# A selective scan with attention and experts behind it: the last direction of three batches is scanned in two halves of the positions, six sums change engine, and ties are drawn from another seed

## The chip, the cores and the metric

One Trainium2 chip, one core. The time is device microseconds (us) of one execution. An execution under the profiler has a time of its own, given below beside the runs without it.

## The reference, cut to what matters

The input is a 4 x 384 x 32 x 32 image; all arithmetic is float32. Layer 0 normalises it in groups and runs a state-space scan over the 1024 positions in four directions (rows forward, columns forward, and both reversed); layer 1 is windowed causal attention and a top-2-of-4 mixture of experts over the 1024 tokens of each batch:

```python
x_dbl = einsum('bkdl,kcd->bkcl', xs, x_proj_weight)      # k: 4 directions
dt = softplus(einsum(..., dts, dt_projs_weight) + bias)
h = h * exp(dt * A) + (dt * u) * B                       # 384 channels x 16 states
y = (h * C).sum(states)                                  # over 1024 positions
x = x + gelu(layernorm(merge of the 4 directions + D * u))
t = t + attention(layernorm(t))                          # 6 heads, window 64, causal
t = t + sum over 2 of 4 experts of gate * (gelu(t @ w1 + b1) @ w2 + b2)
```

The layer norm, and so attention, needs the sum of all four directions at a position. Attention is causal, so the first 512 tokens of a batch don't need the last 512.

## The kernel before, in words

**The scan.** There are 16 turns: four batches of four directions each, in `ORDER` (columns forward, columns reversed, rows forward, rows reversed). A turn has 48 slots. A slot is one tile of 128 partitions (32 channels x 4 states) by 1024 positions; 12 blocks `n` of channels by 4 groups `g` of states make a turn, and `place_of` takes two blocks at a time. For each slot, in the order of `s`:

- `spread` (twice, for the decay and for the input) brings a block's rows of `dtr` from DRAM to 128 partitions, each row copied to four partitions (tiles `dts` and `dtu`; the profile calls both dts);
- `times_b` on GpSimd makes z = dt * u times B;
- `decay` on ScalarE makes dA = exp(scale * dt) into PSUM, of which there are two buffers of this shape;
- `scan` on VectorE runs the recurrence over the 1024 positions, into dA or into z;
- `times_c` multiplies by C, on VectorE or, where the recorder's clocks say that GpSimd is less far along, on GpSimd;
- `fold_y` adds up the 16 states on TensorE with a 128 x 32 matrix of ones, four matmuls for each pair of slots, and adds the result to the rows of `ydr`.

`time_steps` and `half_step` make `dtr` ahead of that: a small matmul, five ScalarE passes and some VectorE passes over 128 x 512 pieces. In the turns of batch 0 (`by_pe`) the three parts of dt are summed by TensorE with an identity matrix; in the others by two VectorE operations.

**Attention.** `layer1` waits until all four directions of a batch have been added (`("scan", b) in have`) and then runs `tokens(b)`: eight tiles of 128 tokens, three at a time, with transposes, norms, projections, scores and outputs on TensorE and copies and norms on ScalarE and VectorE.

**Experts.** `route` orders the tokens of half a batch (four tiles) by expert. The experts' work is 73 blocks of 128 tokens for one expert each, in `hidden` (36 matmuls of 128 x 128 a block, tile ps_hid) and `output` (12 matmuls of 128 x 384 a block, tile y_ff); the profile shows each fp32 matmul as two records. In order of half batches the blocks are 5 and 14 (batch 0), 5 and 8 (batch 1), 8 and 14 (batch 2), 5 and 14 (batch 3). A block can run when its half batch has been routed. `combine` gathers the two experts' rows, weights and adds them and writes the output.

**The order of the work.** The program is straight-line. A recorder (`Machine`) runs these generators against a model of the engines and writes each engine's instructions in the order that it finds; on the chip each engine goes through its list in that order. A request with the bias `EARLY` (the scan's supply, folds, attention, routes) goes ahead of one with `LATER` (experts, combine). Requests that are equal are ordered by a small random amount, from the fixed `SEED`. Nothing is decided at run time but the experts' numbers and the tokens' addresses.

Of the kernel before, what the change touches and what calls it, by code (L numbers as in the profile page):

```python
# [11 lines left out]
F32 = mybir.dt.float32  # L12
AF = mybir.ActivationFunctionType
# [4 lines left out]
P = 128  # L18
# [371 lines left out]


PATIENCE = 3.0
TIE, SEED = 0.1, 53
SOON = 0.5
WINDOW, COLD = 3.413, 1.9
MARGIN, QUEUES = 1.0, ("sp",)
# [4 lines left out]
def conv_attn_hybrid(  # L401
# [88 lines left out]
    count_p = const.tile([P, SEG], F32, name="count_p")  # L490
    base_of = [const.tile([P, NE], F32, name=f"base{n}") for n in range(min(2, len(PACKS)))]
    a4 = const.tile([P, KG, T, JB, NG], F32, name="a4")

    m = Machine(nc)
    ps_a = ctx.enter_context(tc.tile_pool(name="ps_a", bufs=1, space=PSUM))
# [64 lines left out]
    zs, das, ready = {}, {}, set()  # L560
# [4 lines left out]
    def place_of(s):  # L565

        return s // SP * 2 + s % 2, s % SP // 2

    def scans(n):
        return lambda: count_of["scan"] >= n  # L570
# [272 lines left out]
    def time_steps():  # L843

        for i, (b, k) in enumerate(turns):
            for t in range(T):
                yield lambda: i in xds and i in dtws and (i == 0 or ("u", b) in have) and count_of["scan"] >= (i * T + t) * TS - 40
                if i:
                    u = yield from us_all.take("ub")
                    yield from sp.dma_start(u, udr[b][t])  # L850
                else:
                    u = first_u[t][:, :L]
                dtr = dram.tile([2, P, L], F32, tag="dtr", name="dtr", bufs=4)
                halves_ = [half_step(i, t, h, u, dtr) for h in range(NH)]
                yield from m.together(halves_, 1 if b else NH, EARLY)
                if i:
                    us_all.give(u)
                dtrs[i, t] = dtr
            if i == KG - 1:
                own_ = lambda: [f for f in eds.free if f[1].startswith("pt")]  # L860
                yield lambda: len(own_()) == 3
                pts_.free += own_()
                eds.free = [f for f in eds.free if f not in pts_.free]

    def half_step(i, t, h, u, dtr):
        b, k = turns[i]
        bias, c = dtb_sb[:, k, t : t + 1], ts(h, HB)
        by_pe = b == 0
        e, dt, *more = yield from eds.take("ed", n=3 if by_pe else 2)
        w = yield from banks.take("ps_dt", 0)  # L870
        yield from pe.matmul(w, dtws[i][h][:, ts(t, P)], xds[i][h], start=True, stop=True)
        yield from act.activation(e, w, AF.Abs, bias=bias)
        yield from act.activation(dt, w, AF.Relu, bias=bias)
        yield from act.activation(e, e, AF.Exp, scale=-1.0)
        if by_pe:
            yield from act.activation(w, e, AF.Identity, bias=minus, scale=-1.0)
            yield from dve.scalar_tensor_tensor(e, w, 1.0, e, ALU.add, ALU.add)
            yield from act.activation(more[0], w, AF.Ln, scale=-1.0)
            mm = Calls()
            for n, part in enumerate((dt, e, more[0])):  # L880
                mm.matmul(w, ident, part, start=n == 0, stop=n == 2)
            yield from pe.all(mm)
        else:
            yield from act.activation(w, e, AF.Identity, bias=1.0)
            yield from dve.scalar_tensor_tensor(e, w, -1.0, e, ALU.add, ALU.subtract)
            yield from act.activation(w, w, AF.Ln)
            yield from dve.tensor_tensor(w, w, e, ALU.subtract)
            yield from dve.tensor_tensor(w, w, dt, ALU.add)
        if k % 2:
            v = slice(h * (WW // NH), (h + 1) * (WW // NH))  # L890
            yield from dve.tensor_tensor(
                e.rearrange("p (w h) -> p w h", h=HH),
                w.rearrange("p (w h) -> p w h", h=HH), colmajor(u)[:, v, :], ALU.mult,
            )
        else:
            yield from dve.tensor_tensor(e, w, u[:, c], ALU.mult)
        yield from act.copy(dt, w)
        banks.give(w)
        yield from sp.dma_start(dtr[1][:, c], e)
        yield from sp.dma_start(dtr[0][:, c], dt)  # L900
        eds.give(e, dt, *more)

    def spread(c):

        for n, (i, t, j) in enumerate(blocks):
            yield lambda: (i, t) in dtrs
            dst = yield from (dtus if c else dts).take("dts")
            yield from sp.dma_start(
                dst, dtrs[i, t][c, 32 * j : 32 * j + 32, :].unsqueeze(1).to_broadcast([32, SG, L])
            )  # L910
            spreads[n, c] = dst

    def times_b():
        for s in range(NSLOT):
            n, g = place_of(s)
            i = blocks[n][0]
# [4 lines left out]
            yield from pool.tensor_tensor(z, spreads[n, 1], bcs[i, g, 0], ALU.mult)  # L921
            zs[s] = z
            count_of["times"] += 1
            if g == NG - 1:
                dtus.give(spreads.pop((n, 1)))
            if n % NB == NB - 1:
                bs_.give(bcs.pop((i, g, 0)))

    def decay():
        for s in range(NSLOT):  # L930
            n, g = place_of(s)
            i, t, j = blocks[n]
            yield lambda: (n, 0) in spreads and "a4" in have
            da = yield from das_.take("dA")
            yield from act.activation(
                da, spreads[n, 0], AF.Exp, scale=a4[:, turns[i][1], t, j, g : g + 1]
            )
            das[s] = da
            if g == NG - 1:
                dts.give(spreads.pop((n, 0)))  # L940

    def times_c(s, h, on_pool):
        n, g = place_of(s)
        i = blocks[n][0]
        yield lambda: (i, g, 1) in bcs
        if on_pool:
            yield from pool.tensor_tensor(zs[s], zs[s], bcs[i, g, 1], ALU.mult)
        else:
            yield from dve.tensor_tensor(zs[s], h, bcs[i, g, 1], ALU.mult)
            das_.give(h)  # L950
        if n % NB == NB - 1:
            cs_.give(bcs.pop((i, g, 1)))
        ready.add(s)

    def scan():

        for s in range(NSLOT):
            n, g = place_of(s)
            i = blocks[n][0]
# [4 lines left out]
            if turns[i][1] >= 2:  # L964
                yield from dve.tensor_tensor_scan(
                    h[:, ::-1], da[:, ::-1], z[:, ::-1], 0.0, ALU.mult, ALU.add
                )
            else:
                yield from dve.tensor_tensor_scan(h, da, z, 0.0, ALU.mult, ALU.add)
            count_of["scan"] = s + 1  # L970
            if s % SP == 0:
                m.spawn(fold_y(n), EARLY)
            if on_pool:
                das_.give(da)
                m.spawn(times_c(s, h, True))
            else:
                yield from times_c(s, h, False)
# [11 lines left out]
    def fold_y(n):  # L989


        i, t, j = blocks[n]
        b, k = turns[i]
        rows_y = ydr[b][t, j : j + 2].rearrange("j r l -> (j r) l")
# [77 lines left out]
    def tokens(b):  # L1072
# [241 lines left out]
    def route(at_part):  # L1314
# [67 lines left out]
        nb = rp.tile([P, NE], F32, tag="nb", name="nb")  # L1382
        slot = rp.tile([P, PT, NE], F32, tag="slot", name="slot", bufs=1)
        if opens:
            total = rp.tile([P, NE], F32, tag="total", name="total")
            done = rp.tile([P, NE], F32, tag="done", name="done")
            start = rp.tile([P, NE], F32, tag="start", name="start")
# [325 lines left out]
```

## Time and profile before

| | |
|---|---|
| three runs | 3725.29, 3725.83 and 3727.22 us; median 3725.83 us |
| profiled execution | 3715.52 us; span of the core 3713.8 us; mean granted TensorE clock 0.852 |
| busy in the span | TensorE 2999.4 us (81%), VectorE 2858.1 (77%), GpSimd 2802.2 (75%), ScalarE 2217.3 (60%) |
| DMA | 944.51 MB, mean 254 GB/s |

The span has three stages. Up to about 740 us only the scan of batch 0 and its preparation run. From there to the last scan's end, at 3030 us, the scans of batches 1 to 3 run beside the attention and the experts of the batches before. After that only attention of batch 3, the experts that are left and the output remain; VectorE and GpSimd are nearly idle there.

In the pages and answers, a group's line gives engine, operation, tile written and tiles read, and count, then busy us and mean ns of one; a window's line gives each engine's busy us and instructions in that stretch, the granted TensorE clock as a share of full speed, the share of the DMA engines that was busy and their GB/s. L155 and L166 are the recorder's own lines, through which nearly all instructions go, so instructions are told apart by their tiles.

### The profile page before, as it was taken

To read this page: it belongs to the slowest core of one execution; us is meant where nothing else is said; L and a number is where in the kernel's file an instruction comes from. 1 tells how busy PE (TensorE), PEld (TensorE's weight loads), DVE (VectorE), ACT (ScalarE), POOL (GpSimd) and SP (SyncE) were. 2 spreads that over 40 slices of the span, in tenths; PEclk is the share of its full clock that TensorE was granted. 3 is DMA by queue.
4 is the path that set the end of the run, shared out by engine and by line. 5 is a ranking of instruction groups with operands and counts; after the bars stand their busy time and mean duration, and the time that the engine had idled before them with its cause. 6 is when DMAs were issued, how large, how long until landed. Compare 5 with 4: busy or idle time off the path is not lost.

```text
span 3713.8 us, 49879 instructions
## 1 busy us (share of the span) xinstructions
PE 2999.4 (81%) x15793; PEld 1820.8 (49%) x15793; DVE 2858.1 (77%) x3282; ACT 2217.3 (60%) x3984; POOL 2802.2 (75%) x1466
## 2 busy tenths in 40 slices
PE   5566565578788888896778898988888889999997
PEld 2111110045455545463445555655555558877886
DVE  4999999989888999999888999898898963331001
ACT  4454455477676777775667577876667644542221
POOL 3999988989899988999888799998899950112001
PEclk8766776688799989896778899987999999999997
DMA  5876887635489988864369999553899874469995
GB/s 201 288 279 238 276 301 251 207 124 165 150 298 347 368 323 329 304 211 151 124 218 311 328 338 347 194 178 133 291 320 328 321 262 156 153 222 321 321 322 174
DMA packets 396472, 944.51 MB, mean 254 GB/s; under 512 B 50064, under 2 KB 181256, under 8 KB 396208
## 3 DMA queue, kind: packets, MB, share of 16 engines
q1 hardware_dynamic: 384600, 915.73, 70.7%
q0 software_dynamic: 8192, 25.17, 2.0%
q8 instruction: 126, 2.06, 0.2%
q14 instruction: 138, 1.13, 0.1%
q10 hardware_dynamic: 3416, 0.41, 0.1%
HBM read 765.26 MB, written 194.77 MB: 259 GB/s over the span
## 4 chain that ended last, share of the span: by engine, by line
PE 34%; DVE 14%; ACT 10%; POOL 8%; DMA 7%; issue 6%; SPq 1%; another core or an unknown queue 1%; DVEq 0%; POOLq 0%; ACTq 0%
PE y_ff L166 9%; PE ps_hid L166 9%; POOL z L155 6%; DVE dA L155 5%; DVE z L155 4%; PE ps_y L166 3%; PE ps_qk L166 3%; ACT dA L155 2%; PE ps_pr L166 2%; DMA dtr<-ed 2%; PE ps_o L166 2%; ACT ed L155 1%; DVE ps_r L166 1%; PE ps_c L166 1%; ACT L166 1%
## 5 line engine op out<-in xcount | busy, mean ns | idle before, releaser
L155 POOL TENSOR_TENSOR z<-dts,bc 128x1024 f32<-128x1024 f32 x768 | 1792.9, 2363 | 112.5 <-PE ps_y L166 55.7
L155 ACT ACTIVATE dA<-dts,a 128x1024 f32<-128x1024 f32 x768 | 855.3, 1118 | 500.5 <-DVE z L155 486.0
L155 DVE TENSOR_TENSOR_SCAN dA<-dA,z 128x1024 f32<-128x1024 f32 x418 | 955.9, 2287 | 88.9 <-ACT dA L155 75.1
L166 PE MATMUL ps_y<-z,fold 128*32 128x512 f32 x3072 | 665.9, 732 | 321.4 <-POOL z L155 177.1
L155 POOL TENSOR_TENSOR z<-z,bc 128x1024 f32<-128x1024 f32 x350 | 821.3, 2360 | 106.7 <-DVE z L155 105.3
L155 DVE TENSOR_TENSOR_SCAN z<-dA,z 128x1024 f32<-128x1024 f32 x350 | 786.3, 2275 | 38.3 <-ACT dA L155 36.2
L166 PE MATMUL y_ff<-w_sb,hs 128*128 128x384 f32 x1752 | 671.1, 524 | 49.7 <-ACT hs L166 48.6
L166 PEld LDWEIGHTS ps_hid<-xbt,w_sb 128*128 128x128 f32 x5256 | 634.5, 196 | 131.0 <-issue 47.5
L166 PE MATMUL ps_hid<-xbt,w_sb 128*128 128x128 f32 x5256 | 658.8, 282 | 23.1 <-DMA w_sb<-wl 6.7
L155 DVE TENSOR_TENSOR z<-dA,bc 128x1024 f32<-128x1024 f32 x418 | 510.3, 1221 | 19.1
L166 PEld LDWEIGHTS y_ff<-w_sb,hs 128*128 128x128 f32 x1752 | 333.9, 204 | 297.9 <-ACT hs L166 72.9
L155 ACT ACTIVATE hs<-ps_hid,bb 128x128 f32<-128x128 f32 x876 | 262.0, 365 | 337.8 <-PE ps_hid L166 249.6
L166 PEld LDWEIGHTS ps_y<-z,fold 128*32 128x32 f32 x3072 | 91.6, 118 | 694.6 <-POOL z L155 322.9
L155 POOL DMA_INDIRECT cb<-ysdr,idx x64 | 61.9, 967 | 311.8 <-DMA ysdr<-yb 277.1
L166 POOL TENSOR_TENSOR rn<-rn,half 128x1 f32<-128x1 f32 x96 | 53.1, 553 | 229.6 <-DVE rn L166 188.3
L155 DVE COPY yb<-y_ff 128x384 f32<-128x384 f32 x23 | 12.8, 557 | 243.6 <-PE y_ff L166 242.0
L155 POOL DMA_INDIRECT xsdr<-tks,idx x64 | 65.4, 1022 | 110.0 <-DVE idx L166 48.2
L155 ACT ACTIVATE ed<-ps_dt,dtb_sb 128x512 f32<-128x512 f32 x192 | 123.5, 681 | 38.0 <-PE ps_dt L155 24.1
L155 ACT COPY ed<-ps_dt 128x512 f32<-128x512 f32 x96 | 56.2, 585 | 116.0 <-DVE ed L155 115.8
L166 PE MATMUL ps_dt<-ed,ident 128*128 128x512 f32 x144 | 82.7, 729 | 45.0 <-ACT ed L155 45.0
L155 PE MATMUL ps_dt<-xd,dtw_sb 12*128 12x512 f32 x180 | 108.7, 780 | 9.3 <-DVE gate L166 3.0
L311 ACT ACT_TABLE_LOAD x79 | 101.4, 1283 | 13.0 <-DMA gb_sb<-in_gb_dram 11.6
(220 smaller groups left out, 3509.8 us busy)
## 6 DMA issues: line engine op xcount, KB each, us to landing
w_sb<-wl SPq DMA_DIRECT2D x584, 576.0 KB
dts<-dtr SPq DMA_DIRECT2D x384, 512.0 KB
bc<-xdr SPq DMA_DIRECT2D x128, 512.0 KB
dtr<-ed SPq DMA_DIRECT2D x192, 256.0 KB
yp<-ydr SPq DMA_DIRECT2D x96, 256.0 KB
ydr<-yp SPq DMA_DIRECT2D x96, 256.0 KB
ub<-udr SPq DMA_DIRECT2D x45, 512.0 KB
xsdr<-zero SPq DMA_DIRECT2D x12, 1536.0 KB
```

Of the source, the lines that this page charges most:

```text
L155: return getattr(self.real, op)(*a, **k)
L166: getattr(self.real, op)(*a, **k)
L311: self.nc.scalar.add_instruction(mybir.InstLoadActFuncSet(name=self.nc.get_next_instruction_name(), act_func_set_id=EXP_LN_SET,))
```

## The change

Turns 7, 11 and 15, the last of batches 1, 2 and 3, are scanned in two parts (`halved`): all 384 channels over positions 0 to 511, then all of them over 512 to 1023. A slot still covers 128 partitions and 1024 columns, but these are two blocks of channels by 512 positions. Such a slot has two scans of 512, two exponentials of 512, and spreads of two half-rows each; the state at position 511 is kept in `carry` (a copy of two columns) and is the second part's start. The last direction must then run forward, so `ORDER` ends with rows forward. `layer1` starts a batch when its first 512 positions are complete, and each tile waits for its own half. The six sums of the first piece of the first turn (`by_pe`, i + t = 0) are made by VectorE. The seed for ties is 46, and three small routing tiles have one buffer.

```diff
-TIE, SEED = 0.1, 53
+TIE, SEED = 0.1, 46
...
+    carry = [const.tile([P, 2 * NG], F32, name=f"carry{n}") for n in range(NB // NH)]
...
-    ORDER = (1, 3, 0, 2)
+    ORDER = (1, 3, 2, 0)
...
+    halves = [(c, t, j) for c in range(NH) for t in range(T) for j in range(0, JB, 2)]
+    halved = (7,11,15)
...
+    def what(n):
+        i, t, j = blocks[n]
+        if i not in halved:
+            return i, None, t, j
+        return i, *halves[n - i * NB]
...
+    def rows_of(i, g, c, hf):
+        bc = bcs[i, g, c]
+        return bc if hf is None else bcast(bc[:, ts(hf, HB)], 2)
+    def kept(n, g):
+        return carry[n % NB % (NB // NH)][:, 2 * g : 2 * g + 2].unsqueeze(2)
...
-        by_pe = b == 0
+        by_pe = b == 0 and i + t > 0
...
+            else:
+                for o in range(2):
+                    r = slice(32 * (j + o), 32 * (j + o) + 32)
+                    yield from sp.dma_start(
+                        dst[:, ts(o, HB)],
+                        dtrs[i, t][c, r, ts(hf, HB)].unsqueeze(1).to_broadcast([32, SG, HB]),
+                    )
...
+            for o in range(1 if hf is None else 2):
+                c = slice(0, L) if hf is None else ts(o, HB)
+                yield from act.activation(
+                    da[:, c], spreads[n, 0][:, c], AF.Exp,
+                    scale=a4[:, turns[i][1], t, j + o, g : g + 1],
+                )
...
+        eng = pool if on_pool else dve
+        if hf == 0:
+            yield from eng.tensor_copy(kept(n, g), pairs(h)[:, :, HB - 1 : HB])
+        yield from eng.tensor_tensor(view(zs[s], hf), view(h, hf), rows_of(i, g, 1, hf), ALU.mult)
...
+            if hf is not None:
+                for o in range(2):
+                    c = ts(o, HB)
+                    initial = kept(n, g)[:, o, :] if hf else 0.0
+                    yield from dve.tensor_tensor_scan(h[:, c], da[:, c], z[:, c], initial, ALU.mult, ALU.add)
...
-        folded[b] = folded.get(b, 0) + 2
-        if folded[b] == KG * NB:
-            have.add(("scan", b))
+        key = b, hf
+        folded[key] = folded.get(key, 0) + 1
+        whole = (KG - (i // KG * KG + KG - 1 in halved)) * NB // 2
+        for c in range(NH):
+            if folded[b, None] == whole and (whole == KG * NB // 2 or folded.get((b, c), 0) == NB // 4):
+                have.add(("scan", b, c))
...
         def tile(a):
+            yield lambda: ("scan", b, a // PT) in have
...
-            yield lambda: ("scan", b) in have
+            yield lambda: ("scan", b, 0) in have
             yield from tokens(b)
```

More of the change, by code (lines that the diff above doesn't have):

```diff
@@ L567, in place_of, with pairs, view @@
         return s // SP * 2 + s % 2, s % SP // 2
+    def what(n):
[3 more added lines that the diff above has]
+        return i, *halves[n - i * NB]
+    def pairs(ap):
+        return ap.rearrange("p (o l) -> p o l", o=2)
+    def rows_of(i, g, c, hf):
+        bc = bcs[i, g, c]
+        return bc if hf is None else bcast(bc[:, ts(hf, HB)], 2)
+    def view(ap, hf):
+        return ap if hf is None else pairs(ap)
+    def kept(n, g):
+        return carry[n % NB % (NB // NH)][:, 2 * g : 2 * g + 2].unsqueeze(2)
     def scans(n):
@@ L846, in time_steps @@
             for t in range(T):
-                yield lambda: i in xds and i in dtws and (i == 0 or ("u", b) in have) and count_of["scan"] >= (i * T + t) * TS - 40
+                first = i * IS + t * TS // (2 if i in halved else 1)
+                yield lambda: i in xds and i in dtws and (i == 0 or ("u", b) in have) and count_of["scan"] >= first - 40
                 if i:
@@ L903, in spread @@
     def spread(c):
-        for n, (i, t, j) in enumerate(blocks):
+        for n in range(len(blocks)):
+            i, hf, t, j = what(n)
             yield lambda: (i, t) in dtrs
             dst = yield from (dtus if c else dts).take("dts")
-            yield from sp.dma_start(
-                dst, dtrs[i, t][c, 32 * j : 32 * j + 32, :].unsqueeze(1).to_broadcast([32, SG, L])
-            )
+            if hf is None:
+                yield from sp.dma_start(
+                    dst, dtrs[i, t][c, 32 * j : 32 * j + 32, :].unsqueeze(1).to_broadcast([32, SG, L])
+                )
+            else:
+                for o in range(2):
+                    r = slice(32 * (j + o), 32 * (j + o) + 32)
+                    yield from sp.dma_start(
+                        dst[:, ts(o, HB)],
+                        dtrs[i, t][c, r, ts(hf, HB)].unsqueeze(1).to_broadcast([32, SG, HB]),
+                    )
             spreads[n, c] = dst
@@ L915, in times_b @@
             n, g = place_of(s)
-            i = blocks[n][0]
+            i, hf, *_ = what(n)
             yield lambda: (
@@ L920, in times_b @@
             z = yield from zs_.take("z", 0)
-            yield from pool.tensor_tensor(z, spreads[n, 1], bcs[i, g, 0], ALU.mult)
+            yield from pool.tensor_tensor(
+                view(z, hf), view(spreads[n, 1], hf), rows_of(i, g, 0, hf), ALU.mult
+            )
             zs[s] = z
@@ L931, in decay @@
             n, g = place_of(s)
-            i, t, j = blocks[n]
+            i, hf, t, j = what(n)
             yield lambda: (n, 0) in spreads and "a4" in have
             da = yield from das_.take("dA")
-            yield from act.activation(
-                da, spreads[n, 0], AF.Exp, scale=a4[:, turns[i][1], t, j, g : g + 1]
-            )
+            for o in range(1 if hf is None else 2):
[3 more added lines that the diff above has]
+                    scale=a4[:, turns[i][1], t, j + o, g : g + 1],
+                )
             das[s] = da
@@ L943, in times_c @@
         n, g = place_of(s)
-        i = blocks[n][0]
+        i, hf, *_ = what(n)
         yield lambda: (i, g, 1) in bcs
[L946 to L949, printed above, removed]
+        eng = pool if on_pool else dve
+        if hf == 0:
+            yield from eng.tensor_copy(kept(n, g), pairs(h)[:, :, HB - 1 : HB])
+        yield from eng.tensor_tensor(view(zs[s], hf), view(h, hf), rows_of(i, g, 1, hf), ALU.mult)
+        if not on_pool:
             das_.give(h)
@@ L958, in scan @@
             n, g = place_of(s)
-            i = blocks[n][0]
+            i, hf, *_ = what(n)
             yield lambda: s in zs and s in das
@@ L963, in scan @@
             h = z if on_pool else da
-            if turns[i][1] >= 2:
+            if hf is not None:
[3 more added lines that the diff above has]
+                    yield from dve.tensor_tensor_scan(h[:, c], da[:, c], z[:, c], initial, ALU.mult, ALU.add)
+            elif turns[i][1] >= 2:
                 yield from dve.tensor_tensor_scan(
@@ L989, in fold_y @@
     def fold_y(n):
-        i, t, j = blocks[n]
+        i, hf, t, j = what(n)
         b, k = turns[i]
-        rows_y = ydr[b][t, j : j + 2].rearrange("j r l -> (j r) l")
+        if hf is None:
+            rows_y = ydr[b][t, j : j + 2].rearrange("j r l -> (j r) l")
+        else:
+            rows_y = ydr[b][t, :, 32 * hf : 32 * hf + 32, :]
         yield lambda: ("yd", b, t) in have and "fold" in have
@@ L1384, in route @@
         if opens:
-            total = rp.tile([P, NE], F32, tag="total", name="total")
-            done = rp.tile([P, NE], F32, tag="done", name="done")
-            start = rp.tile([P, NE], F32, tag="start", name="start")
+            total = rp.tile([P, NE], F32, tag="total", name="total", bufs=1)
+            done = rp.tile([P, NE], F32, tag="done", name="done", bufs=1)
+            start = rp.tile([P, NE], F32, tag="start", name="start", bufs=1)
             counts[PACK[b]] = total, done, start
```

## The prediction

> **What bounds the kernel now.** I read the busy times in windows of 50 us first: stages have different limits.
>
> ```profile
> core 0: us, PE busy (x) PEld busy (x) DVE busy (x) ACT busy (x) POOL busy (x), PEclk, DMA share, GB/s
> 1200.00:1250.00 50.00, 46.86 (x274) 29.80 (x274) 45.94 (x46) 36.22 (x59) 49.37 (x23) 0.99 0.93 344
> ...
> 1700.00:1750.00 50.00, 30.76 (x98) 13.47 (x98) 46.37 (x40) 30.73 (x40) 49.39 (x28) 0.50 0.45 147
> ...
> 3500.00:3550.00 50.00, 50.00 (x308) 40.07 (x307) 1.67 (x3) 11.91 (x40) 0.00 (x0) 1.00 0.93 316
> ```
>
> Until 3030 us VectorE (DVE) and GpSimd (POOL) are both over 90% busy in most windows: they set the scan's pace. After it TensorE (PE) alone is full. So the end is the last scan's end, 3030 us, plus the TensorE work still left then, 684 us. The same windows for y_ff show which expert work fills TensorE:
>
> ```profile
> 1500.00:1550.00 50.00, 17.32 (x48) 8.47 (x48) 0.00 (x0) 0.95 (x2) 0.96 0.94 337
> ...
> 1700.00:1750.00 50.00, 0.00 (x0) 0.00 (x0) 0.00 (x0) 0.00 (x0) 0.50 0.45 147
> ...
> 3500.00:3550.00 50.00, 26.32 (x76) 13.12 (x74) 1.67 (x3) 0.00 (x0) 1.00 0.93 316
> ```
>
> Experts run at 1050 to 1650, 1950 to 2400 and from 2600 on. Between, all blocks that have been routed are used up and the next batch's attention is still under way: TensorE is 61% busy at half clock at 1700. Expert work missing from these two holes is done after 3030. That is what the change can move.
>
> Then the groups, for the scan's prices, and the waits:
>
> ```profile
> L155 ACT ACTIVATE dA<-dts,a 128x1024 f32<-128x1024 f32 x768 | 855.3, 1118 | 500.5 <-DVE z L155 486.0
> L155 DVE TENSOR_TENSOR_SCAN dA<-dA,z 128x1024 f32<-128x1024 f32 x418 | 955.9, 2287 | 88.9 <-ACT dA L155 75.1
> ...
> L155 DVE TENSOR_TENSOR_SCAN z<-dA,z 128x1024 f32<-128x1024 f32 x350 | 786.3, 2275 | 38.3 <-ACT dA L155 36.2
> ```
>
> ```profile
> PE ps_y L166 <- POOL z L155: 177.1, 92, 7.1
> PE ps_y L166 <- DVE z L155: 131.3, 76, 4.4
> ```
>
> The scan waits 111 us in all for ScalarE (ACT), that is 0.15 us a slot; folds on TensorE wait 308 us for products.
>
> **1. What moves, by the built order.** The instruction order of both programs can be counted without running them. Ahead of the last fold on TensorE stand 46.25 blocks of y_ff and 47.25 of ps_hid before, 50.0 and 51.0 after: 3.75 more. Attention matmuls of all kinds amount to 24.0 tiles there before, 25.2 after. By half-turns: the first three tiles of batch 1 move from turn 8 into turn 7, no experts stand in turns 9.0 and 9.5 before, 4 blocks after, and batch 1's eight tiles end a full turn earlier. The hole of batch 2 stays two half-turns long but lies one half-turn earlier (12.0 and 12.5 instead of 12.5 and 13.0).
>
> Price of a block after 3030 us: from 3450 to 3650 TensorE does nothing else; the y_ff windows there hold 76 + 76 + 74 + 78 = 304 records, at 24 a block 12.7 blocks in 200 us: 15.8 us. Price of a tile: 684 us less 26.3 blocks x 15.8 = 415, the last 46 us (output after the last block) and 16 combined tiles x 2.45 (the two ps_c rows, 78.5 us for 32) = 39 leaves 184 us for 8 tiles, 23 us each. So the work left falls by 3.75 x 15.8 + 1.2 x 23 = 59 + 28 = **87 us**.
>
> **2. What the moved work costs the scan.** I took the start of every 24th of the 768 scans in the timeline. With nothing beside (turns 0.5 to 3.5) a half-turn takes 81.4 us in the mean; with three blocks beside (6.0 to 7.5, 11.0, 11.5, 14.0, 14.5) 88.9, so 2.5 us a block; with attention of batch 0 (4.0 to 5.0; 7.8 tiles) 315.6, so (315.6 - 244.2 - 2)/7.8 = 8.9 us a tile, of batch 2 (12.0 to 13.5) about 10. The moved work costs 3.75 x 2.5 + 1.2 x 9.5 = **21 us** of later scan end.
>
> **3. What the two parts cost.** 144 slots (3 turns) get a second scan. No scan of 512 is in the trace. Additions of 1024 (1221 ns) against 512 (685, rows of yp and ps_dt) give 2 x 685 - 1221 = 149 ns for one more instruction; scans back to back start every 2.21 us where one alone takes 2.29, which puts the lower end at 80 ns. At 149: 21 us of VectorE. Copies of the state: 46 on VectorE (0.16 us, the row of 128x3 from PSUM: 7 us) and 26 on GpSimd (between 0.19 and 0.55 us, rows of rn; 5 to 14 us). Three products move to GpSimd: +7 us there, -4 on VectorE. An initial value read from a tile instead of a constant is in no row: 0 to 149 ns for each of 144 scans, 0 to 21 us; I take 0, since the VectorE rows whose scalar is a tile (tensor_scalar on rn, 153 ns) are no dearer than others. Together 24 us on VectorE and 17 on GpSimd; these two share the products by their loads, so half the sum, 21 us, if the sharing holds, and 13 to 45 at the ends.
>
> ScalarE: 288 exponentials of 512 for 144 of 1024. Rows of 512 take 0.60 to 0.63, so 2 x 0.61 - 1.12 = 0.10 us a slot, 14 us, nearly all beside the scan (ScalarE is 70 to 75% busy, and idles 486 us waiting for buffers that VectorE frees). But VectorE is queued behind this, so 3 us of it counts. Together **24 us**.
>
> The 72 spreads become 144 with half the bytes each: 72 more issues at 0.52 us on SP's queue, 37 us over 530 us of halved turns; weights and folds' rows are queued behind them. SP's waits are for producers, and spreads run ahead by four buffers, so I take 0. If that cover is gone, a late weight stops ps_hid, which waited 6.7 us for weights in all: up to 10 us. In the trace's packet records, packets of 2048 bytes take 84 ns (median) and of 4096 bytes 159: the same per byte, so nothing is added. *The Trainium skill, "Perfetto Trace Analysis", section "DMA Optimizations", speaks against the change here: it says that batching from 2 KB to 4 KB "can dramatically improve throughput", and the change goes the other way. The packet rows don't bear that out; by the rule the sum would rise, as the third rival works out.*
>
> **4. First sums by VectorE.**
>
> ```profile
> 36.11 7.37 PE L166 MATMUL ps_dt<-ed,ident 128*128 128x512 f32 x12 [2.94 <-ACT ed L155]
> ...
> 40.95 1.03 DVE L155 TENSOR_TENSOR ed<-ps_dt,xn 128x512 f32<-128x512 f32 x1 [2.79 <-PE ps_dt L166]
> ```
>
> The first product waits until 40.95 for TensorE. Two VectorE additions (0.69 each) after the logarithm's end at 36.1 give 37.5. VectorE's other small work of this moment (a, count, base) costs half a us. All of the first spread, which GpSimd waits 35 us for, follows: **-3 us**.
>
> **5. The seed.** It reorders near-equal requests all over the program; its large effects are in the counts of part 1. What is left is put in the range, +-10 us.
>
> **Sum.** Scan's end 3030 - 3 + 21 + 24 = 3072; work behind it 684 - 87 = 597; span 3669, which is 45 less. The profiled execution (3715.5) was 10 us under the median of the other runs; the same difference taken from 3725.8 gives about **3681 us**.
>
> **Rivals.**
> - *Slower: the halved turns starve for dA.* A half-slot needs two exponentials, then two scans, with only two buffers between ScalarE and VectorE, and time steps for all three channel tiles of such a turn fall into its first half. If VectorE stands for six tenths of 1.22 us in each of 144 slots, 105 us stand in place of the 24: 3681 + 81 = 3762. It decides from (45 + 24)/144 = 0.48 us a slot. For it: the 111 us of waits for dA. Against: they are 0.15 us a slot.
> - *Nothing gained: TensorE no longer full behind the scan.* Before the last route of batch 3, 8.25 blocks of y_ff fill gaps between 8 tiles behind the last scan; after, 5 between 6.8 tiles. If a chain of tiles (three at a time, about 75 us from rows to token) sets the pace, half of the 87 is lost: 3725. Against: 5 x 15.8 + 6.8 x 23 = 235 us of work is more than 2.3 rounds x 75 = 170.
> - *Slower: packets.* Spreads of halved turns are 72 x 128 packets of 4 KB, at 187 ns (mean) and over 16 DMA engines 108 us. If halves cost as much as wholes, 108 us are added where the DMA share is 0.85 to 1.0: 3681 + about 70 = 3751. Against: the packet rows.
> - *Faster: the second scans hide.* If the pair overlaps (80 ns), VectorE's added work goes where it stood waiting, and experts in former gaps cost the scan nothing: 10 in place of 45 us: 3646.
>
> **Chances.** Forecast 0.59, faster rival 0.17, nothing gained 0.09, starved 0.12, packets 0.03. About 7.5 us (0.2%) is what a measurement tells from no change. Faster by more than that: 0.59 + 0.17 and a little of "nothing gained", 0.78; within 0.07; slower 0.15. The range runs from the faster rival to just beyond no change, 3645 to 3735; the likeliest case's own is 3663 to 3712, from the unknown costs (-8; +21 and a late weight's 10) and the seed's 10.
>
> **What would show it.** Right: the last scan ends at 3060 to 3085; y_ff windows fill around turn 9 (1700 to 1800 before) and the clock there rises from 0.50; about 23 blocks behind the last scan and some 600 us; 512 scans at 1.2 us; half-turns in turns 7, 11, 15 at 3 to 7 us over their like before. Wrong: scans waiting for dA by well over 111 us; TensorE below 90% between the last scan and the last route; a scan's end after 3110.

## The result and the profile after

The changed kernel takes 3712.1 us (median of 16 runs, 3703.3 to 3721.9), the kernel before 3726.2 us (16 runs, 3710.3 to 3740.3): a ratio of 0.9963, 95% interval 0.9951 to 0.9974. That is 14 us faster, where 45 were forecast. The profiled executions can't show these 14: that of before was 10.6 us under its median, that of after, 3717.15 us (span 3715.4), 5.0 us above its own. Executions of the kernel after lie up to 10 us from their median, of the one before up to 16; a scan's end read from one profile is meant with that error throughout. The chips of e9 to e18 were 0.4% faster for the kernel before too (3711 against 3727 us), so kernels are compared by their ratios. Scan's end and the us behind it from e7 are multiplied by 0.9956 where they stand beside those chips'. That is an assumption: a scan of 1024 takes 2.28 us in the mean on every one of them, so the scan's stage need not shrink by the same share.

In the spans, the last scan ends at 3110.9 us (before: 3029.6; forecast: 3072), and 604.5 us of work follow it (before: 684.2; forecast: 597). The gain behind the scan came as forecast; the scan lost twice what was forecast.

The windows of after that answer to those of before:

```profile
core 0: us, PE busy (x) PEld busy (x) DVE busy (x) ACT busy (x) POOL busy (x), PEclk, DMA share, GB/s
1200.00:1250.00 50.00, 46.89 (x258) 28.62 (x258) 42.63 (x40) 40.85 (x67) 46.58 (x22) 0.93 0.94 334
1700.00:1750.00 50.00, 41.41 (x198) 28.79 (x197) 42.65 (x111) 31.05 (x63) 34.29 (x22) 0.69 0.61 196
3500.00:3550.00 50.00, 50.00 (x305) 39.80 (x304) 1.68 (x3) 12.45 (x42) 0.00 (x0) 1.00 0.93 319
```

and for y_ff alone:

```profile
core 0: us, PE busy (x) PEld busy (x) DVE busy (x) ACT busy (x), PEclk, DMA share, GB/s
1500.00:1550.00 50.00, 6.51 (x18) 3.18 (x18) 0.00 (x0) 0.00 (x0) 1.00 0.78 260
1700.00:1750.00 50.00, 6.20 (x12) 3.16 (x12) 0.00 (x0) 0.00 (x0) 0.69 0.61 196
1800.00:1850.00 50.00, 10.11 (x24) 4.90 (x24) 0.00 (x0) 0.47 (x1) 0.93 0.71 233
3500.00:3550.00 50.00, 26.89 (x78) 13.42 (x76) 1.68 (x3) 0.00 (x0) 1.00 0.93 319
```

At 1700 us TensorE is now 41 of 50 us busy (31 before), at a granted clock of 0.69 instead of 0.50; half a block of y_ff stands in a window that had none, a whole one at 1800. At 1500, where 48 records of y_ff stood, there are now 18. From 3500 on the stage behind the scan is as full as it was. VectorE, 92% busy at 1200 us before, is 85% busy there now; but that window lies in turn 6, which isn't halved, and turns 4 to 6 take 594.4 us from scan start to scan start (before: 598.3). The loss is not there.

What the two parts are made of, in the groups by form (count, then busy us and mean ns of one):

```profile
L155 ACT ACTIVATE dA<-dts,a 128x512 f32<-128x512 f32 x288 | 197.2, 691 | 75.4 <-DVE z L155 70.8
...
L155 DVE TENSOR_TENSOR_SCAN dA<-dA,z 128x512 f32<-128x512 f32 x92 | 112.8, 1226 | 26.9 <-issue 9.3 <-ACT dA L155 8.1 <-POOL z L155 4.4
...
L155 DVE TENSOR_TENSOR_SCAN z<-dA,carry,z 128x512 f32<-128x512 f32 x82 | 100.2, 1265 | 1.5 <-ACT dA L155 1.5
...
L155 DVE TENSOR_TENSOR_SCAN dA<-dA,carry,z 128x512 f32<-128x512 f32 x62 | 79.6, 1285 | 14.8 <-ACT dA L155 5.7 <-POOL z L155 5.2 <-issue 3.0
...
L155 DVE TENSOR_TENSOR_SCAN z<-dA,z 128x512 f32<-128x512 f32 x52 | 59.7, 1202 | 1.4 <-ACT dA L155 0.9 <-DMA w_sb<-wl 0.5
...
L155 DVE COPY carry<-dA 128x2 f32<-128x2 f32 x46 | 7.3, 158 | 1.4
...
L155 POOL COPY carry<-z 128x2 f32<-128x2 f32 x26 | 5.0, 193 | 24.8 <-DVE z L155 24.8
```

The 288 scans of 512 take 352.3 us; 144 of 1024 at 2.28 us would take 329. So VectorE has 23.5 us more of scans and 7.3 of copies (forecast: 21 and 7), GpSimd 5.0 of copies (5 to 14). The exponentials of 512 are dearer than forecast: 691 ns instead of 0.61 us, 197.2 us in place of 144 x 1.118 = 161, so 36 us and not 14 on ScalarE.

The waits (total us, times, longest us):

```profile
PE ps_y L166 <- POOL z L155: 168.0, 72, 7.4
...
PE ps_y L166 <- DVE z L155: 116.6, 66, 5.1
...
DVE dA L155 <- ACT dA L155: 70.8, 49, 4.5
...
DVE z L155 <- ACT dA L155: 32.6, 25, 5.2
```

The scan's waits for dA come to 103 us, against 111 before, and to 16 us in the three halved turns alone, against 15: the halved turns don't starve for it, as the first rival had it. Nor did the folds wait longer (285 us, before 308).

Where, then, does the scan lose? In the halved turns. Half-turns (24 slots) in us, from the starts of the scans; "whole slots" is e6 and "not halved" e5, both below:

| half-turn | before | after | whole slots | not halved |
|---|---|---|---|---|
| 7, first | 87.1 | 102.8 | 85.9 | 86.8 |
| 7, second | 88.6 | 106.6 | 103.9 | 87.9 |
| 11, first | 89.1 | 99.1 | 89.2 | 91.5 |
| 11, second | 85.8 | 108.9 | 102.0 | 88.5 |
| 15, first | 74.8 | 88.4 | 79.9 | 76.2 |
| 15, second | 75.6 | 99.5 | 90.4 | 75.6 |
| sum | 501.1 | 605.3 | 551.2 | 506.5 |

No attention of the batch can stand in the first halves, and yet they are 15.7, 10.0 and 13.6 us longer than before; 3 to 7 were forecast. Turn 7's first half in the windows, before and then after:

```profile
core 0: us, PE busy (x) PEld busy (x) DVE busy (x) ACT busy (x) POOL busy (x), PEclk, DMA share, GB/s
1317.30:1404.40 87.10, 77.99 (x398) 43.41 (x397) 82.49 (x56) 59.91 (x97) 72.33 (x31) 0.91 0.86 306
```

```profile
core 0: us, PE busy (x) PEld busy (x) DVE busy (x) ACT busy (x) POOL busy (x), PEclk, DMA share, GB/s
1316.40:1419.10 102.70, 87.78 (x447) 50.79 (x445) 85.55 (x94) 74.96 (x139) 78.68 (x42) 0.93 0.92 320
```

15.6 us more time, but only 3.1 more of work on VectorE and 6.4 on GpSimd. VectorE's idle time rises from 4.6 to 17.2 us, GpSimd's from 14.8 to 24.0. This half-turn is long because both engines that carry the scan wait more, not because they do more. That doesn't hold for all six: a table below has VectorE's busy and idle time for them together.

The first product, in the timeline of after (start, duration):

```profile
36.80 0.69 DVE L155 TENSOR_TENSOR ps_dt<-ps_dt,ed 128x512 f32<-128x512 f32 x1
...
38.20 1.00 DVE L155 TENSOR_TENSOR ed<-ps_dt,xn 128x512 f32<-128x512 f32 x1
```

It starts at 38.2 instead of 40.95, and the first scan at 57.8 instead of 61.1 us. The gain doesn't last: turn 4 starts at 721.9 us, 3 us later than before (719.0).

### The profile page after: what moved, and what is told of

The parts are those of the page before. It is cut to its first block, busy times and chain, and to the rows that moved or that the text cites. A ratio compares the mean times of both kernels' runs of the same rounds, so it can differ in the third digit from the quotient of the medians.

```text
span 3715.4 us, 50370 instructions
## 1 busy us (share of the span) xinstructions
PE 2983.6 (80%) x15787; PEld 1821.7 (49%) x15787; DVE 2877.4 (77%) x3455; ACT 2264.4 (61%) x4174; POOL 2814.8 (76%) x1495
## 4 chain that ended last, share of the span: by engine, by line
PE 28%; DVE 10%; DMA 8%; ACT 8%; POOL 6%; issue 4%; SPq 1%; another core or an unknown queue 1%; POOLq 0%; DVEq 0%; ACTq 0%
PE ps_hid L166 8%; PE y_ff L166 8%; POOL z L155 5%; DVE dA L155 3%; DVE z L155 3%; PE ps_y L166 2%; ACT dA L155 2%; PE ps_o L166 1%; DMA xb<-xsdr 1%; PE ps_pr L166 1%; DMA w_sb<-wl 1%; PE ps_qk L166 1%; PE ps_c L166 1%; SPq L155 1%; DMA dtr<-ed 1%
## 5 line engine op out<-in xcount | busy, mean ns | idle before, releaser
L155 ACT ACTIVATE dA<-dts,a 128x1024 f32<-128x1024 f32 (+1 forms) x912 | 892.0, 983 | 485.5 <-DVE z L155 470.1
L155 DVE TENSOR_TENSOR_SCAN dA<-dA,z 128x1024 f32<-128x1024 f32 (+1 forms) x430 | 885.7, 2060 | 88.0 <-ACT dA L155 65.1
L166 PE MATMUL ps_y<-z,fold 128*32 128x512 f32 x3072 | 641.7, 716 | 299.9 <-POOL z L155 168.0
L155 DVE TENSOR_TENSOR_SCAN z<-dA,z 128x1024 f32<-128x1024 f32 (+1 forms) x338 | 702.9, 2111 | 32.0 <-ACT dA L155 31.1
L166 PEld LDWEIGHTS ps_hid<-xbt,w_sb 128*128 128x128 f32 x5256 | 643.4, 198 | 142.1 <-issue 41.0
L166 PE MATMUL ps_hid<-xbt,w_sb 128*128 128x128 f32 x5256 | 667.9, 284 | 30.6 <-issue 6.2
L155 DVE TENSOR_TENSOR ps_dt<-ps_dt,ed 128x512 f32<-128x512 f32 x148 | 102.4, 692 | 16.7 <-ACT ps_dt L155 14.8
```

Of the source, the lines that this page charges most:

```text
L155: return getattr(self.real, op)(*a, **k)
L166: getattr(self.real, op)(*a, **k)
```

## The experiments

**The small instructions, with the order kept (e1, e2, e3).** Each engine's list keeps the order of after; only what stands in the halved turns' places is exchanged: the recorder is asked for the old instruction and writes the whole one (or none). e2 does this for the exponentials, e3 for scans and copies, e1 for all and the spreads.

```diff
+    def swap(self, op, a, k, put):
+        yield self.ask(op, a, k)
+        if put:
+            op, a, k = put
+            getattr(self.real, op)(*a, **k)
...
-                yield from act.activation(
-                    da[:, c], spreads[n, 0][:, c], AF.Exp,
-                    scale=a4[:, turns[i][1], t, j + o, g : g + 1],
+                kw = dict(scale=a4[:, turns[i][1], t, j + o, g : g + 1])
+                whole_ = ("activation", (da, spreads[n, 0], AF.Exp), kw)
+                yield from act.swap(
+                    "activation", (da[:, c], spreads[n, 0][:, c], AF.Exp), kw, None if o else whole_
```

e1: 

> The changed kernel with every engine's list in the same order, but in turns 7, 11 and 15 one exponential and one scan of 1024 stand where two of 512 stood, one spread of a whole row where two of half rows, and no copy of the state (the result of these turns is left wrong by that). Theory A, the two parts' own instructions are what holds the scan up (its end 82 us later than before in the profiles, 42 in the prediction): the last scan ends 50 to 65 us earlier than in the changed kernel, near 3050, and the time is 45 to 65 us under it. Theory B, the new order is what holds it up (folds, time steps and attention's first tiles crowded into these turns): the last scan ends less than 20 us earlier and the time falls by less than 20.

e2: 

> The changed kernel in the same order, but with one exponential of 1024 for two of 512 in turns 7, 11 and 15 (the second block's decay is left wrong by that). A pair takes 2 x 691 ns in the changed kernel's profile where one took 1118, not 1220 as predicted: 38 us of ScalarE. If VectorE's wait for dA is what the halved turns lose, the last scan ends 20 to 40 us earlier; if ScalarE's work lies beside the scan, as predicted, under 8 us.

e3: 

> The changed kernel in the same order, but with one scan of 1024 for two of 512 in turns 7, 11 and 15, and without the copies of the state (the recurrence is left wrong by that). The pairs cost 144 x about 0.2 us and the copies 7 us on VectorE and 5 on GpSimd. As predicted (half of that shows): the last scan ends about 20 us earlier and the time is 15 to 20 less. If VectorE alone sets the pace there: 35 us. If the order does: under 8.

Measured: e1 0.9932 [0.9915, 0.9949], six half-turns 592.2 us; e2 0.9965 [0.9949, 0.9982], 605.1; e3 0.9990 [0.9976, 1.0003], 606.5. All of the added instructions together give back 13 of the 104 us in the half-turns, and some 0.3% of the time; exponentials alone give nothing, and scans and copies alone made it slower than after, for which I have no explanation. Read by themselves, these runs would say that the cut is nearly free. They say only that little of its price comes back once the order is fixed: in the halved turns of e1 VectorE is busy 27 us less than in after, but idle 14 us more, and its waits for dA rise from 16 to 38 us.

**What the early attention is worth (e4).** Attention waits for both parts; the turns stay halved.

```diff
-            yield lambda: ("scan", b, 0) in have
+            yield lambda: ("scan", b, 0) in have and ("scan", b, 1) in have
```

> The changed kernel, in which a batch's attention starts only when both parts are complete: halved turns without what they are for (planned anew). The work behind the last scan should be that of before, about 684 us, and the scan's end shows what the two parts cost without attention's tiles in them. By the prediction's price, 24 us: the time is 3740 to 3755, 20 to 30 above the kernel before. If the two parts cost some 65 us, as the profile of the changed kernel suggests: 3775 to 3800.

Measured: 1.0212 [1.0190, 1.0235]; the scan ends at 3092.3, and 698.5 us follow. The work behind the scan is not less than before: the 80 us gained there come from the early attention. e4 also shows the price of the two parts by itself. With 45.5 blocks and 24 tiles ahead of the last fold it has moved no work to speak of (e5, without halves: 46.25 and 24), and its scan still ends 60 us after e5's (3032.0). By its ratio e4 takes 3805 us: near what the expectation had for a price of some 65 us (3775 to 3800), and far from that for 24.

**No halves, and whole slots in the halves' order (e5, e6).** Both are planned anew by the recorder. e5 keeps the seed, the sums by VectorE and the new `ORDER`. e6 keeps the halved turns' slots, waits and early attention, but a slot has one exponential, one scan, one spread of each kind and no copy.

```diff
 # e5
-    halved = (7,11,15)
+    halved = ()
 # e6
-            if hf is None:
+            if True:
                 yield from sp.dma_start(
...
-            for o in range(1 if hf is None else 2):
-                c = slice(0, L) if hf is None else ts(o, HB)
+            for o in range(1):
+                c = slice(0, L)
...
-        if hf == 0:
+        if False:
             yield from eng.tensor_copy(kept(n, g), pairs(h)[:, :, HB - 1 : HB])
...
-            if hf is not None:
+            if False:
                 for o in range(2):
```

e5: 

> The changed kernel with no turn in two parts; the new order of directions, the sums by VectorE and the seed 46 stay. Ahead of the last fold stand 46.25 blocks and 24 tiles, as in the kernel before. If the seed and the sums are worth what the prediction gave them (-3 and +-10): 3715 to 3735. If the whole gain of 14 us is the seed's: near 3712.

e6: 

> The changed kernel planned anew with whole slots: in turns 7, 11 and 15 one exponential, one scan and one spread of 1024 as elsewhere and no copy of the state, but folds, blocks' order and attention's start as in the changed kernel (the result of these turns is left wrong). 49.0 blocks and 26.5 tiles stand ahead of the last fold. In the run with the same order but whole slots the halved half-turns hardly got shorter. If what they lose comes from how the small instructions were placed between others when the order was written, they come down here to 83 to 92 us (7.0, 11.0) and 76 to 82 (15.0), the scan ends near 3060 and the time is 3670 to 3690, as predicted for the change. If it comes from the new order of blocks, from folds or from attention's early start, they stay near 100 and 88 and the time is above 3700.

Measured: e5 0.9973 [0.9960, 0.9986], scan's end 3032.0, 685.1 us behind it. e6 0.9883 [0.9865, 0.9902], 3054.0 and 626.8. So seed, sums and the new order of directions alone give 10 us, and halving adds 4. The order with halves is worth its forecast gain, and the cut of the instructions takes most of it: 57 us at the scan's end (3110.9 - 3054.0), 30 us in the time. (e6 has 49.0 blocks ahead of the last fold, after 50.0: one block more lies behind its scan, and the 57 hold what that block costs the scan.) Of the 57, 54 lie in the six half-turns of the table. Turn 7's first half in the windows of e6:

```profile
core 0: us, PE busy (x) PEld busy (x) DVE busy (x) ACT busy (x) POOL busy (x), PEclk, DMA share, GB/s
1316.00:1402.00 86.00, 79.30 (x420) 46.06 (x423) 81.09 (x53) 60.59 (x100) 74.40 (x33) 0.94 0.94 335
```

VectorE idles 4.9 us here and 17.2 in after, while TensorE is 92% busy here and 85% in after, and the DMA share is 0.94 and 0.92. With the order of halves and the experts beside it, but whole instructions, the scan doesn't wait like that: the longer waits go with the cut and the order that was planned around it.

**Is that the seed? (e7, e13 to e17).** The same three programs under seeds 53 (the old one) and 1.

```diff
-TIE, SEED = 0.1, 46
+TIE, SEED = 0.1, 53
```

e7: 

> The changed kernel with the seed of the kernel before. 49.25 blocks and 26 tiles stand ahead of the last fold, 0.75 block and some tiles short of seed 46: by the prediction's prices 12 us more behind the scan. If the seed is worth no more than +-10: 3705 to 3725. If halved turns are slow by an accident of seed 46, their half-turns are much shorter here and the time is under 3700.

e13: 

> Whole slots in turns 7, 11 and 15 planned anew, as in the run of that name under seed 46 (the result of these turns is left wrong), but under seed 53. If the split's price is its own: the same 0.8% (29 us) under the halved kernel of seed 53, so a ratio near 0.993, with turn 7.0, 11.0 and 15.0 at 85 to 90, 85 to 90 and 76 to 80 us. If it was an accident of seed 46: a ratio of 0.998 or more.

e14: 

> No turn in two parts, sums by VectorE, new order of directions, seed 53: 43.75 blocks and 24 tiles ahead of the last fold, 2.5 blocks fewer than before. By the price of a block the work behind the scan is 40 us more, so a ratio near 1.010 if TensorE is full behind the scan; then halving is worth 0.9% under this seed. If the counts do not decide: near 1.000.

e15: 

> The changed kernel under seed 1: 49.0 blocks and 26.5 tiles ahead of the last fold. If the split's price is its own: the first halves of halved turns 10 to 16 us over the kernel before (turn 7.0 near 100, 11.0 near 99, 15.0 near 88), a scan's end near 3110, and a ratio of 0.996 to 1.002. If accident: one or two of the three near their whole length.

e16: 

> Whole slots in turns 7, 11 and 15 planned anew under seed 1 (the result of these turns is left wrong). If the split's price is its own: 0.6 to 1.0% under the halved kernel of seed 1. If accident: within 0.3% of it.

e17: 

> No turn in two parts, seed 1: 47.25 blocks and 24 tiles ahead of the last fold, a block more than in the kernel before. By the price of a block: 16 us less behind the scan, a ratio near 0.996 if the scan ends as before. Halving under this seed is then worth nothing or is a loss, as its 1.75 blocks and 2.5 tiles more (28 + 58 us) stand against some 70 us of scan.

Measured, as ratio to the kernel before (intervals of +-0.001 to 0.002), then scan's end and the us behind it:

| seed | not halved | halved | whole slots |
|---|---|---|---|
| 46 | 0.9973; 3032.0, 685.1 | 0.9963; 3110.9, 604.5 | 0.9883; 3054.0, 626.8 |
| 53 | 1.0164; 3043.8, 725.5 | 1.0013; 3104.7, 604.8 | 0.9933; 3067.4, 614.3 |
| 1 | 1.0012; 3041.1, 669.2 | 1.0030; 3119.2, 611.0 | 0.9951; 3082.9, 616.9 |
| mean | 1.0050 | 1.0002 | 0.9922 |

The cut costs 0.80, 0.80 and 0.79% (each known to 0.2 to 0.3%): 30 us at every seed, so it is no chance of one order. Where in the halved turns it falls does depend on the order. Under seed 1 the first halves take 95.4, 87.0 and 84.5 us, where e15's expectation had about 100, 99 and 88, and the second half of turn 11 takes 120.4. With whole slots under seed 53 they take 93.7, 92.1 and 76.8 (expected: 85 to 90, 85 to 90 and 76 to 80). But the six together are close. The three halved turns under each seed, in us as measured; the waits are the scans' for dA:

| seed, slots | length | VectorE busy | VectorE idle | waits for dA |
|---|---|---|---|---|
| before | 501.1 | 473.8 | 27.2 | 15 |
| 46, halved (after) | 605.3 | 515.5 | 89.7 | 16 |
| 46, whole slots (e6) | 551.2 | 487.8 | 63.4 | 26 |
| 53, halved (e7) | 605.9 | 515.2 | 90.6 | 19 |
| 53, whole slots (e13) | 561.8 | 494.7 | 67.1 | 32 |
| 1, halved (e15) | 603.2 | 511.3 | 92.0 | 20 |
| 1, whole slots (e16) | 560.2 | 486.5 | 73.7 | 36 |

The cut makes these turns 54, 44 and 43 us longer. Of that 28, 21 and 25 us are work of VectorE, and 26, 24 and 18 its idle time. And VectorE waits less for the exponentials with the cut than without it, under each seed. What it waits for more is, by the profile's releasers, TensorE's results in ps_y (9, 23 and 7 us), GpSimd's z (10 and 13 us under seeds 46 and 1) and "issue" (12, 9 and 5), that is, nothing that the profile shows.

The halved program is 0.1% faster, 1.5% faster and 0.2% slower than the one that isn't halved: what the change brings depends on the seed as much as on the halves. The programs without halves scatter by 1.9%, by what is left behind the scan: 46.25, 43.75 and 47.25 blocks of y_ff stand ahead of the last fold, and 685.1, 725.5 and 669.2 us follow. From 47.25 to 43.75 that is 56.3 us for 3.5 blocks, 16.1 each; the prediction's price was 15.8. The halved programs scatter by 0.7%. e7 and e15 are slower than was expected of them (3705 to 3725 us; a ratio of up to 1.002), e14 and e17 too (1.010 and 0.996).

**Turn 15 alone not halved (e8).**

```diff
-    halved = (7,11,15)
+    halved = (7, 11)
```

> The changed kernel with turns 7 and 11 in two parts and turn 15 whole: the same instructions up to turn 13. 50.0 blocks and 24 tiles stand ahead of the last fold. Turn 15's half-turns took 88 and 99 us where the kernel before took 75 and 76: the last scan should end some 30 us earlier, near 3075 to 3085. Work behind it: 684 - 59 = 625 by the prediction's price of a block. Time 3700 to 3715 if TensorE stays full there, so turn 15's halving would be worth nothing or a little; over 3725 if attention of batch 3 without its early start leaves TensorE waiting.

Measured: 1.0094 [1.0077, 1.0110], 49 us slower than after. The scan ends 31 us earlier, at 3080.3, but 690.8 us follow (expected: 625), although 50.0 blocks stand ahead of the last fold as in after. Its windows behind the scan, and then those of after:

```profile
core 0: us, PE busy (x) PEld busy (x) DVE busy (x) ACT busy (x) POOL busy (x), PEclk, DMA share, GB/s
3200.00:3250.00 50.00, 40.38 (x208) 33.06 (x209) 19.29 (x63) 22.53 (x52) 19.87 (x28) 0.74 0.47 137
3300.00:3350.00 50.00, 40.67 (x207) 35.83 (x207) 20.38 (x83) 11.61 (x27) 17.28 (x23) 0.64 0.36 111
```

```profile
core 0: us, PE busy (x) PEld busy (x) DVE busy (x) ACT busy (x) POOL busy (x), PEclk, DMA share, GB/s
3200.00:3250.00 50.00, 49.68 (x357) 43.25 (x356) 27.38 (x128) 24.78 (x72) 4.33 (x8) 0.97 0.38 116
3300.00:3350.00 50.00, 46.20 (x321) 40.21 (x320) 14.92 (x45) 19.55 (x52) 16.84 (x20) 0.95 0.72 230
```

This is the second rival, in e8 and not in after: in these windows TensorE is 81% busy at a clock of 0.64 to 0.74 in e8, 92 to 99% at 0.95 and more in after. From 3100 to 3400 us it is busy 262 of 300 us at 0.81 in e8, 285 at 0.96 in after and 287 at 0.97 before; blocks done earlier are worth nothing in e8. e8 has as few blocks left as after, but all eight tiles of batch 3; that the blocks are too few to stand between these tiles is argued from this, and no run varies it alone.

**Which small instructions (e9, e10), planned anew.** e9 takes of e6's edit only the loop of the exponentials (A is the same for all channels in this input, so one scale serves both blocks, and e2 and e9 leave no decay wrong, other than their expectations say), e10 only the scans and copies.

```diff
 # e9
-            for o in range(1 if hf is None else 2):
-                c = slice(0, L) if hf is None else ts(o, HB)
+            for o in range(1):
+                c = slice(0, L)
 # e10
-        if hf == 0:
+        if False:
...
-            if hf is not None:
+            if False:
```

e9: 

> The changed kernel planned anew with one exponential of 1024 where two of 512 stood in turns 7, 11 and 15; scans, copies and spreads stay in two (the second block's decay is left wrong). Whole slots planned anew ended the scan 57 us earlier (3054 for 3111) and took 29 us off the time, while whole instructions in the old order took off 9. Theory, exponentials: a pair is two requests to ScalarE, between which gelus with their two table loads are put, with only two dA buffers behind: the scan ends 30 us earlier or more and the time is 3685 to 3700. Theory, scans and copies: under 10 us.

e10: 

> The changed kernel planned anew with one scan of 1024 and no copy of the state in turns 7, 11 and 15; exponentials and spreads stay in two (the recurrence is left wrong). Theory, scans and copies: a slot is four or five requests in a row to VectorE and GpSimd where it was two, and at each of them other work that is due goes ahead: the scan ends 30 us earlier or more and the time is 3685 to 3700. Theory, exponentials: under 10 us.

Measured: e9 0.9994 [0.9981, 1.0007], e10 0.9946 [0.9929, 0.9963]. Brought to the chip of after (x 1.0042), their six half-turns take 595 and 583 us: 10 and 22 below after (13 and 25 without that factor), where both with the whole spreads (e6) are 54 below. In the half-turns each kind of small instruction has a share, and neither has it all. By their ratios they take 3724 and 3706 us on the chip of after; neither theory's 3685 to 3700 came. In the time, e9 is even above after (0.9963), and e10 0.17% below: one such step is no larger than what another order does by chance.

**Asked for together (e11, e12, e18).** All instructions stay small. The two exponentials of a slot (e12; e18 with seed 53), or also its two scans, and its copy with the product (e11), become one request of the recorder, so that nothing can come between them on their engine.

```diff
+            mm = Calls()
             for o in range(1 if hf is None else 2):
                 c = slice(0, L) if hf is None else ts(o, HB)
-                yield from act.activation(
+                mm.activation(
...
+            yield from act.all(mm)
```

e11: 

> The changed kernel, result and all, but each pair of exponentials, each pair of scans and each copy with its product is one request to the recorder, so that nothing is put between (planned anew). If placement between other work is what whole slots gain beyond the instructions themselves (20 of 29 us), this gets most of it back: the scan ends near 3075 and the time is 3690 to 3700. If it is the sum of the instructions and of the engine that each lands on, it stays at 3705 to 3720.

e12: 

> The changed kernel, result and all, with each pair of exponentials as one request to the recorder; scans and copies as they were (planned anew; 49.5 blocks and 25.5 tiles stand ahead of the last fold). If gelus between the two exponentials are the loss: 3685 to 3700. If not: 3705 to 3720.

e18: 

> Pairs of exponentials as one request to the recorder, seed 53; 49.0 blocks and 27.0 tiles ahead of the last fold. If the gain of the same kernel under seed 46 (ratio 0.9935) is from the request: 0.3% under the halved kernel of seed 53, so near 0.998. If it was the order's chance: 1.001 or more.

Measured: e11 1.0015 [1.0003, 1.0027]; e12 0.9935 [0.9915, 0.9956]; e18 0.9973 [0.9958, 0.9988]. With the pair of exponentials as one request the halved program is 0.28% faster under seed 46 and 0.40% under 53; with everything in pairs it is 0.5% slower. The first two gains agree, but they are no larger than what another order does (e9 was 0.3% above after), so it isn't shown that they come from the request. e12 computes all that the reference does and is the fastest of such kernels here: 0.65% faster than before, 0.28% than after. By its ratio that is 3702 us, between its two expectations.

## Why the forecast was right in its sign and wrong in its size

- **What bounds it: read too high.** VectorE and GpSimd are both over 90% busy in 24 of the 58 windows of 50 us from 100 to 3000 us before, not in most.
- **The work behind the scan (part 1): right.** 80 us less in the profiles of before and after, 87 forecast; over three seeds, halved against not halved, 81, 121 and 58, mean 87. e4 shows that it comes from the early attention, and the runs without halves confirm the price of a block.
- **What the moved work costs (part 2): right in the mean.** 21 forecast; whole slots against not halved 22, 24 and 42 us of scan's end.
- **What the two parts cost (part 3): the step that failed.** 24 us forecast, with 45 as the upper end. Measured: 60 us with no work moved (e4 against e5), and halved against whole slots 57 us of scan's end under this seed, 37 under 53 (51 without the factor of 0.9956) and 36 under 1. The instructions themselves were sized well but for the exponentials (36 us and not 14). The 21 us for VectorE's and GpSimd's work are near what VectorE's busy time grew by, 28, 21 and 25 us. What was missed is waiting: I gave it 3 us, for ScalarE, and VectorE's idle time in the halved turns grew by 26, 24 and 18 us against whole slots, not in waits for dA but at TensorE's results, GpSimd's products and "issue". I had read "ScalarE is 70 to 75% busy" as cover and let VectorE and GpSimd share the rest; that VectorE, in its fixed order, would stand longer at other engines' results was not in the sum.
- **First sums (part 4): right at the first scan, but worth nothing.** 3.3 us there, 3 forecast; over the runs with these sums the first scan starts at 57.6 to 61.4 us (before: 61.1), and by turn 4 the scan is 3 us later than before, in a new order of directions and of ties.
- **The seed (part 5): too narrow.** +-10 forecast; with halves the three seeds differ by 0.7% (25 us), without by 1.9%.
- **The sum under this seed.** The scan's end came 81 us later instead of 42: 33 from part 3, 1 from part 2, 5 from e5's scan's end (3032.0, where -3 against before was forecast). The work behind it is 7 us short of its forecast. That makes 46; the two profiled executions stood 15 us wider apart than the medians, which leaves 31, the difference between 45 and 14.
- **The sign is in part luck.** 10 of the 14 us come without any halving (e5), and under seeds 53 and 1 the changed kernel takes 1.0013 and 1.0030 of the kernel before: no gain, and a small loss.
- **The rivals.** "Starved for dA" named the right place and a price (0.48 us a slot) that 54/144 = 0.38 in the halved turns doesn't reach, but the wrong wait. "TensorE no longer full" is real in e8; in after, where turn 15 is halved too, it stays away. "Packets": whole spreads, scans and exponentials together are worth 30 us, so the 70 of that rival aren't there; no run has the spreads alone. "The second scans hide" is excluded by the half-turns. *The Trainium skill's rule that the prediction quotes ("Perfetto Trace Analysis", "DMA Optimizations") names no amount; the runs leave it at most these 30 us.*
- **Of the signs named:** 512 scans at 1.2 us, some 600 us behind the scan, TensorE at 95% from 3100 to 3400 and a clock over 0.50 at 1700 came; the last scan within 3060 to 3085 and half-turns 3 to 7 us longer did not, and "a scan's end after 3110" was named as a sign of being wrong.

*The Trainium skill, "VectorE: DVE Perf Modes", section on the TRN2 errata, says of operations that read SBUF, as the scan reads z, that a fixed cost is paid between instructions, so that many small tiles pay it for each. The trace agrees for scans into dA: one of 1024 takes 2.29 us, two of 512 back to back 2.47 (1318.6 us in the timeline of after). Into z six of 512 in a row take 6.86 us (2929.44 us), 2.29 a pair, as one of 1024 does. So that rule gives 0.2 us a slot at most for scans with a constant start, on VectorE alone, less than the 0.38 by which the halved turns grew.*

What stays open is how the added instructions turn into idle time. Removed from a fixed order they return almost nothing (e1: 13 us in the half-turns), left out before planning 54: under this seed, whether their time comes back depends on the order written around them. Which neighbour comes late in it was not found, and pairing them went with a gain for one kind and a loss for all.

## What to carry to other kernels

Splitting an instruction to let a consumer start earlier costs more than the added work of the busiest engine, even where no engine is busy all the time: here VectorE's added work came out in full, about 25 us, and as much again in VectorE's waits for other engines. Where a program's order is written by a planner, take the suspected cost out before planning as well as from the fixed order, and under several seeds; one seed alone would have called halving worth 0.1%, 1.5% or -0.2%.

## What the runs showed of the hardware

- A scan whose start value is read from a tile takes 1265 and 1285 ns, from a constant 1202 and 1226: about 60 ns more, 0 forecast.
- An exponential of 128x512 from SBUF into PSUM takes 691 ns, of 128x1024 1118: 264 ns in each that don't depend on the size, if the time is linear between these two sizes. Two of 128x512 back to back take 1.42 us.
- Behind the scan, TensorE at 81% busy was granted a clock of 0.64 to 0.74 (e8), at 92 to 99% busy one of 0.95 and 0.97 (after). The two don't go together in every window of 50 us: 0.79 at 93% busy in e8 (3350 to 3400), 0.97 at 87% in e5 (3200 to 3250).
